# A graph network layer: the last blocks of edges in halves, and the last 512 nodes through a layer with nodes as rows

## The chip, the cores and the metric

One core of one Trainium2 chip. The time is device microseconds of one execution. The profile is of one execution of the kernel before; its lines give microseconds (us) from the first instruction. Engines: PE (matmul; PEld its weight loads), DVE (vector), ACT (scalar), POOL (here: issues the gathers), SP (issues the other transfers). L229 is line 229 of the kernel before.

## What is computed

8192 nodes of 256 features, 131072 edges with 64 features, sorted by their target. All in 32-bit floats.

```python
ea  = edge_attr @ w_e + b_e                       # 131072 x 256
msg = relu(x[src] + ea)
agg = segment_sum(msg, dst, 8192)
h_local = bn1(relu((x + agg) @ w1 + b1) @ w2 + b2 + x)
h_attn  = bn2(attention in groups of 32 nodes, 4 heads, of x @ in_w.T + in_b, then out_w, out_b, + x)
out = h_local + h_attn
out = out + relu(out @ m_w1 + m_b1) @ m_w2 + m_b2
result = layernorm(x + bn3(out))                  # over the 256 features
```

The three `bn` are a scale and a shift per feature (s1, s2, s3; cA and c3 gather the shifts).

## The kernel before

**Edges.** The edges go in 128 blocks of 1024, a block in 4 groups (h) of two tiles (j) of 128 edges. Per block:
- `gather(b)` (L157, POOL): 8 indirect DMAs fetch the source rows, 128 each, into `xs` (four buffers).
- `load_edges` (L173, SP) and `edge_transpose` (L190, DVE): edge features to `eaT`.
- `edge_products(b)` (L208, PE): 8 matmuls to `pe`, two PSUM pairs of banks (2 groups each, `bank2`, two buffers in all, which the attention scores at L474 use too).
- `edge_messages(b)`: DVE adds `pe` and `xs` (L229, one add for each half of a block, 128x1024), ACT takes the relu (L233). The add frees the PSUM pair and the gather buffer.
- `edge_hot(b)` (L241, DVE): one-hot tiles `oh` of the targets within a group.
- `edge_sums` (L250, PE): 8 matmuls with 32 columns each sum the messages by target to `pw`; ACT copies to `ws` (L263), DVE makes `oh2` (L267).
- `edge_place` (L278, PE; L287, DVE): two matmuls place the sums in a window of nodes and add them to `xT`, the transposed x of the 512 nodes concerned.

**Nodes.** 16 chunks of 512 nodes. `attention_front` and `attention_back` (L432 to L527) don't need the edges. `dense` does: once the last block that reaches a chunk is placed, it runs `w1` (ACT relu, L553), `w2` (DVE, hA, L556), `m_w1` (ACT relu, L562), `m_w2` (DVE, zT, L574), all with features as rows, transposes zT back (L583, PE), adds x (L589), takes mean and variance (L591, L592), the root (L595, ACT) and writes y (L601, L606). The last two chunks are run in parts: 256, 256, then four of 128 nodes.

**Order.** PE's order is fixed when the program is built. Up to block 104 (`TAIL`) it follows a simple loop, with node work in between. From there a small planner runs on estimated times: `came[b]` is when a block's gathers should have come, `added` when its messages should be there, and at each step it takes placing, sums, products or messages if their estimated time has come, or else a step of node work (`work.step`). DVE's and ACT's order is chosen by the build's scheduler, which keeps `edge_messages` behind the instructions in `newest` (so far the latest `ws` and the latest `xT`), by `tc.issue_after`. Each engine executes its own order strictly, and waits where an operand isn't there.

**General path.** If the targets don't fit the windows, a register (`width`) sends every engine into a second path (from L853), a loop over all edges and one over all nodes. With these inputs it is jumped over, at the end.

Of the kernel before, what the change touches and what calls it, by code (L numbers as in the profile page):

```python
# [9 lines left out]
FP = mybir.dt.float32  # L10
# [8 lines left out]
P = 128  # L19
# [5 lines left out]
NH = 4  # L25
# [14 lines left out]
ND = 2  # L40
NV = 26
TAIL = 104
AGG_ROWS = N + 2 * P
TE = 8
RS = 1.0 / (1.0 + 1e-5) ** 0.5
LN_EPS = 1e-5
REST = -1.0
# [25 lines left out]
def gnn_kernel(ctx: ExitStack, tc: tile.TileContext, x, src, dst, edge_attr, w, out):  # L73
# [60 lines left out]
    s12 = const.tile([P, KC], FP, name="s12")  # L134
    cA = const.tile([P, KC], FP, name="cA")
    c3 = const.tile([P, KC], FP, name="c3")

    fast = ExitStack()
    epool = fast.enter_context(tc.tile_pool(name="edge", bufs=1))
# [50 lines left out]
        nc.vector.transpose(eaT, ea[:, QR:].rearrange("p (g d) -> p g d", d=ED)[:, :, :QR])  # L190


    pe_of, msg_of, oh_of, newest = {}, {}, {}, {}

    def edge_products(b, pairs=range(0, NH, 2)):

# [19 lines left out]
        if b + 2 < NB:  # L216
            load_edges(b + 2)

    def edge_messages(b):

        xs = xs_of.pop(b)
        msg = msg_of[b] = epool.tile([P, NH, TJ, C], FP, name="msg", tag="msg", bufs=3)
        n = 2 if b < NB - 1 else 1
        for h in range(0, NH, 2):
            pe = pe_of.pop((b, h))
            for u in range(0, 2, n):
                hs = slice(h + u, h + u + n)
                for js in [slice(0, TJ)] if n == 2 or h + u < NH - 1 else [slice(j, j + 1) for j in range(TJ)]:
                    nc.vector.tensor_add(  # L229
                        msg[:, hs, js].rearrange("p u i c -> p i u c"), pe[:, js, u : u + n, :],  # L230
                        xs[:, hs, js].rearrange("p u i c -> p i u c"),
                    )
                    nc.scalar.activation(msg[:, hs, js], msg[:, hs, js], AF.Relu)  # L233
        between()
# [13 lines left out]
    def group_sums(pw, i, b, turns):  # L248
        for h, j in turns:
# [2 lines left out]
                start=(j == 0), stop=(j == TJ - 1), skip_group_check=True,  # L252
            )

    def edge_sums(blocks):

        n = len(blocks)
        pw = pps.tile([P, 2, C], FP, name="pw", tag="pw", bufs=1)
        for i, b in enumerate(blocks):
            turns = [(h, j) for j in range(TJ) for h in range(NH)]  # L260
            group_sums(pw, i, b, sorted(turns) if b == NB - 1 else turns)
# [271 lines left out]
    def dense(n0, st, pool, bank, a=0, z=CH, own=("h1", "m1", "zT", "y", "")):  # L533
# [16 lines left out]

        h1 = pool.tile([P, KC, w], FP, name="h1", tag=own[0])
        for o in range(KC):
            nc.scalar.activation(h1[:, o, :], layer(w1, KC, o, tT), AF.Relu, bias=v_("b1", o))  # L553
            yield 1.7 * part
        for o in range(KC):
            nc.vector.scalar_tensor_tensor(  # L556
                hA[:, o, :], layer(w2, KC, o, h1), s1[:, o : o + 1], hA[:, o, :], op0=ALU.mult, op1=ALU.add
            )
            yield 1.7 * part
        m1 = pool.tile([P, 2 * KC, w], FP, name="m1", tag=own[1])  # L560
        for o in range(2 * KC):
            nc.scalar.activation(m1[:, o, :], layer(mw1, KC, o, hA), AF.Relu, bias=v_("m_b1", o))  # L562
            yield 1.7 * part
        zT = pool.tile([P, KC, w], FP, name="zT", tag=own[2])
        for o in range(KC):
# [5 lines left out]
        st6 = pool.tile([P, TN, 6], FP, name="st", tag="st" + own[4])  # L571
        mv = pool.tile([P, TN, 2], FP, name="mv", tag="mv" + own[4])
        for o in range(KC):
            nc.vector.scalar_tensor_tensor(  # L574
                zT[:, o, :], layer(mw2, 2 * KC, o, m1), s3[:, o : o + 1], zT[:, o, :], op0=ALU.mult, op1=ALU.add
            )
            yield 3.4 * part
        for t2 in range(0, nt, 2):
            n2 = min(2, nt - t2)
# [29 lines left out]
        yield 0.0  # L609


# [31 lines left out]
    class Work:  # L643
# [5 lines left out]
        def __init__(self, n):  # L649
            self.streams = [[] for _ in range(n)]  # L650
            self.rest, self.turn, self.owed = [0] * n, 0, 0.0
            self.at, self.placed_at = [0.0] * n, 0.0

        def add(self, stream, ready, gen):
            self.streams[stream].append((ready, gen))
# [25 lines left out]

        def step(self, t, until):

            n = len(self.streams)
            for i in [k % n for k in range(self.turn, self.turn + n)]:
                while self.streams[i] and self.streams[i][0][0]() and t >= self.at[i]:
                    d = next(self.streams[i][0][1], None)
                    if d is None:
                        self.streams[i].pop(0)
                        self.at[i] = max(self.at[i], self.placed_at)  # L690
                    elif d == REST:
                        self.at[i] = t + 6.0
                    elif d > 0:
                        t += d
                        self.at[i], self.turn = t + 0.5, (i + 1) % n
# [14 lines left out]
    with tc.manual_schedule(engines={PE}):  # L710
# [9 lines left out]
        for c in range(NCH):  # L720
            st, before, same = chunk[c], chunk[c - 1], chunk[c - 4]
            front = attention_front(c * CH, st, npool, bank)
            if c < 2:
                next(front)
            work.add(
                FRONT,
                lambda c=c, b=before, s=same: (c < 1 or b.get("scores"))
                and (c < 4 or s.get("dense")),
                front,
            )  # L730
            work.add(BACK, lambda s=st: s.get("front"), attention_back(st, npool, bank, bank2))
            if c < NCH - 2:
                work.add(DENSE, summed(c), dense(c * CH, st, npool, bank))
        for i, c, a, z in (
            (DENSE2, NCH - 2, 0, CH // 2), (DENSE, NCH - 2, CH // 2, CH), (DENSE2, NCH - 1, 0, P),
            (DENSE, NCH - 1, P, 2 * P), (DENSE2, NCH - 1, 2 * P, 3 * P), (DENSE, NCH - 1, 3 * P, CH),
        ):
            d = dense(c * CH, chunk[c], npool, bank, a, z, *([OTHER] if i == DENSE2 else []))
# [10 lines left out]
        while b < TAIL:  # L749
# [5 lines left out]
            for i in blocks:  # L755
                if i + 2 < NB:
                    gather(i + 2)
                if 4 <= i < 8:
                    wt, name = ((w1, "w1"), (w2, "w2"), (mw1, "m_w1"), (mw2, "m_w2"))[i - 4]
                    nc.sync.dma_start(wt, w[name].rearrange("(k p) m -> p k m", p=P))  # L760

            if b:
                edge_products(b)
                edge_messages(b)
                next_edges(b + 2)
# [23 lines left out]
            b += 2  # L789

        came = [7.9 + 10.035 * (i + 1) for i in range(NB)]
        t, p, m, s, l = came[b - 2] + 20, b, b, b - 2, b - 2
        added = dict((i, came[i] + 2.0) for i in range(b))
        summed_at, bank_free = {}, t
        work.at = [t] * len(work.streams)
        while l < NB:

            times = [1e9] * 4
            if l < s:
                times[0] = summed_at[l] + 1.5  # L800
            elif s < m:
                times[1] = max(added[s] + 1.2, bank_free)
                if s == NB - 1:
                    times[1] = max(came[s] + 2.2, bank_free)
            if p < NB - 1 and m == p:
                times[2] = added[p - 1]
            if m < p:
                times[3] = came[m]
            if t >= times[0]:
                edge_place(*sums)  # L810
                placed = l
                t += 0.75
                bank_free = work.placed_at = t + 0.7
                l += 1
                if l == NB - 1:
                    edge_products(l, [2])
                    edge_hot(l)
                    t += 1.0
                    p += 1
            elif t >= times[1]:  # L820
                sums = edge_sums([s])
                t += 1.2
                summed_at[s] = t
                s += 1
                if s == NB - 1:
                    edge_products(s, [0])
                    t += 1.0
            elif t >= times[2]:
                if p + 2 < NB:
                    gather(p + 2)  # L830
                edge_products(p)
                next_edges(p + 2)
                edge_hot(p)
                t += 2.1
                p += 1
            elif t >= times[3]:

                with ExitStack() as behind:
                    for i in newest.values():
                        behind.enter_context(tc.issue_after(i))  # L840
                    edge_messages(m)
                added[m] = max(t, came[m], added[m - 1] + 0.5) + 2.0
                m += 1
            elif l == s - 1 == NB - 1:
                t = times[0]
            else:
                t = work.step(t, min(times))
        work.finish()
# [124 lines left out]
```

## Time and profile before

| | us |
|---|---|
| median of three runs (1314.24 to 1318.11) | 1315.99 |
| the profiled execution | 1315.85 |
| its span, first to last instruction | 1314.1 |
| busy: PE, DVE, ACT, POOL | 1198.9, 803.9, 592.0, 975.3 |
| mean granted clock of PE | 0.964 |

A group's line gives the mean of one instruction: message add 1214 ns (128x1024), relu 1054, 512-column matmul 595 (they overlap; one of a run of 32-bit matmuls takes two such records, 0.86 us), y add 686 (128x512), statistics 411, aggregate 170. A line of the timeline gives start, length, engine, line, operation and, in brackets, the idle time before and what ended it. A line of waits gives total, number and longest.

### The profile page before, as it was taken

What the parts mean: (1) busy time and instruction counts of PE and PEld (TensorE: products, weight loads), DVE (VectorE), ACT (ScalarE), POOL (GpSimd) and SP (SyncE); (2) the same over time, 40 slices, a digit from 0 to 9 for tenths busy, and PEclk for the clock granted to TensorE, in tenths of its full rate; (3) what the DMA queues carried; (4) which work ended last, traced back from release to release, by engine and by line L of the source; (5) the groups of instructions that cost most, each with busy time, mean ns of one, the idle gap of its engine ahead of it and who ended that gap; (6) DMA issues with size and microseconds to landing.
All of it is one profiled execution on the core that took longest, in us unless ns stands there. A gap on an engine that the chain in (4) does not pass through costs nothing.

```text
span 1314.1 us, 21073 instructions
## 1 busy us (share of the span) xinstructions
PE 1198.9 (91%) x7683; PEld 722.8 (55%) x7683; DVE 803.9 (61%) x1634; ACT 592.0 (45%) x850; POOL 975.3 (74%) x1032
## 2 busy tenths in 40 slices
PE   5987989999999989898997999889898999989986
PEld 3554646556565555555564555545555555555665
DVE  6567665757566565745746574565647558475663
ACT  2524444454545264443544444354454445453443
POOL 7777777777777777777777777777777777777772
PEclk8989999999999989898999999989899999999998
DMA  9999976677666666665767566576566567665741
GB/s 230 280 328 275 280 216 166 175 188 192 169 182 158 171 181 159 188 163 152 195 163 185 153 185 169 154 186 169 169 170 191 149 168 194 162 168 154 193 135 48
DMA packets 148922, 240.35 MB, mean 183 GB/s; under 512 B 27950, under 2 KB 112204, under 8 KB 148044
## 3 DMA queue, kind: packets, MB, share of 16 engines
q0 software_dynamic: 49152, 134.28, 38.6%
q1 hardware_dynamic: 98572, 104.65, 29.4%
q8 instruction: 62, 1.02, 0.3%
q14 instruction: 48, 0.39, 0.1%
q10 hardware_dynamic: 1088, 0.00, 0.0%
HBM read 222.06 MB, written 16.78 MB: 182 GB/s over the span
## 4 chain that ended last, share of the span: by engine, by line
POOL 34%; PE 31%; issue 16%; DMA 9%; DVE 8%; ACT 2%; SPq 0%; DVEq 0%; POOLq 0%; ACTq 0%
POOL xs L157 34%; PE at L546 8%; DMA xs<-xb,srci 6%; PE pe L208 6%; PE at L443 3%; PE pw L250 3%; PE pe L203 2%; PE at L524 2%; DVE msg L229 2%; PE l L278 1%; DVE bd L504 1%; PE at L512 1%; PE at L457 1%; DMA xb<-xp 1%; DVE eaT L190 1%
## 5 line engine op out<-in xcount | busy, mean ns | idle before, releaser
L157 POOL DMA_INDIRECT xs<-xb,srci x864 | 819.1, 948 | 263.2 <-issue 247.7
L233 ACT ACTIVATE msg<-msg 128x1024 f32<-128x1024 f32 (+1 forms) x259 | 270.0, 1046 | 401.4 <-DVE msg L229 397.4
L229 DVE TENSOR_TENSOR msg<-pe,xs 128x1024 f32<-128x1024 f32 (+1 forms) x259 | 306.6, 1207 | 196.5 <-PE pe L208 91.2
L208 PE MATMUL pe<-we,eaT 64*128 64x256 f32 x2048 | 270.3, 401 | 13.5 <-ACT pr L484 9.8
L208 PEld LDWEIGHTS pe<-we,eaT 64*128 64x128 f32 x2048 | 195.4, 194 | 117.9 <-issue 62.8
L157 POOL DMA_INDIRECT xs<-in_x_dram,srci x144 | 138.8, 964 | 43.9 <-issue 40.8
L250 PE MATMUL pw<-msg,oh 128*32 128x256 f32 x2048 | 129.8, 385 | 1.2 <-ACT msg L233 0.8
L546 PE MATMUL at<-hA,mw 128*128 128x512 f32 (+2 forms) x320 | 125.8, 520 | 4.5 <-DVE hA L556 4.3
L443 PE MATMUL at<-xT,inT 128*128 128x512 f32 x256 | 121.8, 602 | 3.2 <-ACT xT L433 3.2
L546 PE MATMUL at<-m,mw 128*128 128x512 f32 (+2 forms) x320 | 119.4, 517 | 0.0
L190 DVE STREAM_TRANSPOSE eaT<-ea 128x512 f32<-128x512 f32 x128 | 90.0, 703 | 22.0 <-PE pe L208 18.6
L250 PEld LDWEIGHTS pw<-msg,oh 128*32 128x32 f32 x2048 | 59.9, 110 | 63.6 <-issue 22.8
L278 PEld LDWEIGHTS l<-oh,ws 128*128 128x128 f32 x512 | 73.7, 195 | 27.3 <-issue 21.4
L278 PE MATMUL l<-oh,ws 128*128 128x160 f32 (+4 forms) x512 | 85.9, 308 | 1.8 <-ACT ws L263 1.7
L546 PEld LDWEIGHTS at<-hA,mw 128*128 128x128 f32 x320 | 55.1, 192 | 53.4 <-issue 41.2
L546 PEld LDWEIGHTS at<-m,mw 128*128 128x128 f32 x320 | 55.7, 192 | 48.0 <-issue 44.8
L443 PEld LDWEIGHTS at<-xT,inT 128*128 128x128 f32 x256 | 46.9, 191 | 57.4 <-issue 47.6
L446 ACT ACTIVATE qk<-at,vec 128x512 f32<-128x512 f32 x64 | 43.8, 685 | 73.7 <-PE at L443 73.6
L546 PE MATMUL at<-xT,w 128*128 128x512 f32 (+2 forms) x160 | 66.3, 551 | 8.8 <-DVE xT L287 8.8
L562 ACT ACTIVATE m<-at,vec 128x512 f32<-128x512 f32 (+2 forms) x80 | 47.9, 599 | 58.5 <-PE at L546 58.0
L546 PE MATMUL at<-h,w 128*128 128x512 f32 (+2 forms) x160 | 65.3, 532 | 9.4 <-ACT oT L519 7.0
L241 DVE TENSOR_TENSOR oh<-iota_n,rel 128x128 f32<-128x128 f32 x256 | 57.6, 279 | 18.2 <-PE pw L250 14.8
(111 smaller groups left out, 1200.7 us busy)
## 6 DMA issues: line engine op xcount, KB each, us to landing
ea<-in_edge_attr_dram SPq DMA_DIRECT2D x512, 128.0 KB
xs<-xb,srci POOLq DMA_INDIRECT x864
xn<-in_x_dram SPq DMA_DIRECT2D x16, 512.0 KB
out_dram<-y SPq DMA_DIRECT2D x14, 512.0 KB
xp<-in_x_dram SPq DMA_DIRECT2D x10, 512.0 KB
xb<-xp SPq DMA_DIRECT2D x10, 512.0 KB
xp<-in_x_dram SPq DMA_DIRECT2D x3, 1024.0 KB
xb<-xp SPq DMA_DIRECT2D x3, 1024.0 KB
```

Source lines behind the costliest of these rows:

```text
L157: nc.gpsimd.indirect_dma_start(out=xs[:, h, j, :], out_offset=None, in_=x if b < NX else xb[:, :], in_offset=bass.IndirectOffsetOnAxis(ap= ...
L190: nc.vector.transpose(eaT, ea[:, QR:].rearrange("p (g d) -> p g d", d=ED)[:, :, :QR])
L208: nc.tensor.matmul(pe[:, i, u, :], eaT[rows, h + u], we[rows, :], start=(b >= NX), stop=True, skip_group_check=True)
L229: nc.vector.tensor_add(msg[:, hs, js].rearrange("p u i c -> p i u c"), pe[:, js, u : u + n, :], xs[:, hs, js].rearrange("p u i c -> p i u c"),
L233: nc.scalar.activation(msg[:, hs, js], msg[:, hs, js], AF.Relu)
L241: nc.vector.tensor_tensor(oh[:, ts], iota_n[:, None, :WN].to_broadcast([P, TB // 2, WN]), rel[:, b, ts, None].to_broadcast([P, TB // 2, WN ...
L250: nc.tensor.matmul(pw[h * WN : (h + 1) * WN, i, :], oh_of[b][:, h * TJ + j, :], msg_of[b][:, h, j, :], start=(j == 0), stop=(j == TJ - 1), ...
L278: nc.tensor.matmul(l2[:, k, at : at + wn], ws[:, i, k * P : (k + 1) * P], oh2[:, i, :wn], start=(i == 0 and k == 0), stop=(i == last), ski ...
L443: nc.tensor.matmul(ps, inT[:, k, o * P : (o + 1) * P], xT[:, k, :], start=(k == 0), stop=(k == KC - 1))
L446: nc.scalar.activation(qk[:, o, :], ps, AF.Identity, bias=v_("in_b", o))
L546: nc.tensor.matmul(ps, wt[:, k, o * P : (o + 1) * P], act[:, k, :], start=(k == 0), stop=(k == nk - 1))
L562: nc.scalar.activation(m1[:, o, :], layer(mw1, KC, o, hA), AF.Relu, bias=v_("m_b1", o))
```

## The change

From block 104 on the planner goes by halves of a block: products, messages and sums of two groups at a time, each with its own due time, messages tried ahead of products. `newest` also holds the latest relu and the latest dense step on DVE. Node work is held to a share of 0.42 of the time between blocks 115 and 124. The last part of chunk 14 is two parts of 128 nodes. The last chunk goes through `dense_rows`: up to the third layer as before, then the fourth layer has the activations as stationary operand, so that nodes are rows; x and the bn3 scale enter by matmuls with `ident` and a diagonal into the same PSUM tile, and statistics and output read PSUM. For that `m_w2` is scaled by s3 once, at block 12 (with c3 as a row), and `dense` adds instead of scaling. In the general path the loop over edges takes one tile a turn. SP's last transfers stand in another order: the output of the first 128 nodes of chunk 14's second half is issued ahead of the last block's last edge load.

```diff
-TE = 8
+SHARE = 0.42
+TE = 1
-    def edge_messages(b):
+    def edge_messages(b, pairs=range(0, NH, 2)):
 ...
-        for h in range(0, NH, 2):
+        for h in pairs:
             pe = pe_of.pop((b, h))
 ...
+    def some_sums(b, groups):
+        if b not in pw_of:
+            pw_of[b] = pps.tile([P, 2, C], FP, name="pw", tag="pw", bufs=1)
+        group_sums(pw_of[b], 0, b, [(h, j) for h in groups for j in range(TJ)])
 ...
     (dense)
-            nc.scalar.activation(h1[:, o, :], layer(w1, KC, o, tT), AF.Relu, bias=v_("b1", o))
+            newest["relu"] = nc.scalar.activation(h1[:, o, :], layer(w1, KC, o, tT), AF.Relu, bias=v_("b1", o)).ins
 ...
-            nc.vector.scalar_tensor_tensor(
-                zT[:, o, :], layer(mw2, 2 * KC, o, m1), s3[:, o : o + 1], zT[:, o, :], op0=ALU.mult, op1=ALU.add
-            )
+            newest["dense"] = nc.vector.tensor_add(zT[:, o, :], layer(mw2, 2 * KC, o, m1), zT[:, o, :]).ins
 ...
+    def dense_rows(n0, st, pool, bank, a, own=("h1", "m1", "zT", "y", ""), ahead=False):
 ...
+        nc.vector.tensor_add(y, st["xn"][:, a // P, :], c3row)
+        def sum_of_x():
+            ps = bank()[:, :C]
+            nc.tensor.matmul(ps, ident, y, start=True, stop=False, skip_group_check=True)
+            return ps
 ...
+        for k in range(KC):
+            nc.tensor.matmul(
+                out_ps[:, k * P : (k + 1) * P], hA[:, k, :], diag[:, k, :], start=False, stop=False,
+                skip_group_check=True,
+            )
+        for k in range(2 * KC):
+            nc.tensor.matmul(
+                out_ps, m1[:, k, :], mw2[:, k, :], start=False, stop=(k == 2 * KC - 1), skip_group_check=True
+            )
+        nc.vector.bn_stats(st6, out_ps)
+        nc.vector.bn_aggr(mv, st6)
+        nc.scalar.activation(rstd, mv[:, 1:2], AF.Sqrt, bias=eps_t)
+        nc.vector.reciprocal(rstd, rstd)
+        nc.vector.tensor_scalar(y, out_ps, mv[:, 0:1], rstd, ALU.subtract, ALU.mult)
+        nc.sync.dma_start(out[ds(n0 + a, P), :], y)
 ...
     (Work.step)
+            if self.paced_from <= t < self.paced_to:
+                self.credit += SHARE * (t - max(self.seen, self.paced_from))
+                self.seen = t
+                if self.credit < -0.02:
+                    return min(until, t - self.credit / SHARE)
 ...
     (the parts of the last chunks)
-            (DENSE2, NCH - 2, 0, CH // 2), (DENSE, NCH - 2, CH // 2, CH), (DENSE2, NCH - 1, 0, P),
+            (DENSE2, NCH - 2, 0, CH // 2), (DENSE, NCH - 2, CH // 2, 3 * P), (DENSE, NCH - 2, 3 * P, CH),
+            (DENSE2, NCH - 1, 0, P),
 ...
     (the planner)
-            if l < s:
-                times[0] = summed_at[l] + 1.5
-            elif s < m:
-                times[1] = max(added[s] + 1.2, bank_free)
+            if l < s[0]:
+                times[0] = summed_at[l] + 0.7
+            elif (s[0], s[1] + (s[0] == NB - 1)) < tuple(m):
+                i, k = s
+                times[1] = max(added[i, k] + 1.2, bank_free)
 ...
-            if p < NB - 1 and m == p:
-                times[2] = added[p - 1]
-            if m < p:
-                times[3] = came[m]
+            if p[0] < NB and (p[0] - 1, p[1]) < tuple(m):
+                times[2] = added[p[0] - 1, p[1]]
+            if tuple(m) < tuple(p):
+                times[3] = came[m[0]] - 2.5 * (1 - m[1])
 ...
             elif t >= times[3]:
                 with ExitStack() as behind:
                     for i in newest.values():
                         behind.enter_context(tc.issue_after(i))
-                    edge_messages(m)
-                added[m] = max(t, came[m], added[m - 1] + 0.5) + 2.0
+                    edge_messages(m[0], (2 * m[1],))
+                added[tuple(m)] = max(t, came[m[0]] - 2.5 * (1 - m[1])) + 1.3
 ...
+            elif t >= times[2]:
+                i, k = p
+                if not k and i + 2 < NB:
+                    gather(i + 2)
+                edge_products(i, (2 * k,))
+                if k:
+                    next_edges(i + 2)
+                else:
+                    edge_hot(i)
+                t += 1.0
```

More of the change, by code (lines that the diff above doesn't have):

```diff
@@ L136, in gnn_kernel @@
     c3 = const.tile([P, KC], FP, name="c3")
+    diag = const.tile([P, KC, P], FP, name="diag")
+    c3row = const.tile([P, C], FP, name="c3row")
     fast = ExitStack()
@@ L253, in group_sums @@
             )
+    def some_sums(b, groups):
+        if b not in pw_of:
+            pw_of[b] = pps.tile([P, 2, C], FP, name="pw", tag="pw", bufs=1)
+        group_sums(pw_of[b], 0, b, [(h, j) for h in groups for j in range(TJ)])
     def edge_sums(blocks):
         n = len(blocks)
[L258 to L261, printed above, removed]
+        pw = pw_of.pop(blocks[0], None)
+        if pw is None:
+            pw = pps.tile([P, 2, C], FP, name="pw", tag="pw", bufs=1)
+            for i, b in enumerate(blocks):
+                group_sums(pw, i, b, [(h, j) for j in range(TJ) for h in range(NH)])
         ws = epool.tile([P, 2, C], FP, name="ws", tag="ws", bufs=2)
@@ L561, in dense @@
         for o in range(2 * KC):
-            nc.scalar.activation(m1[:, o, :], layer(mw1, KC, o, hA), AF.Relu, bias=v_("m_b1", o))
+            newest["relu"] = nc.scalar.activation(m1[:, o, :], layer(mw1, KC, o, hA), AF.Relu, bias=v_("m_b1", o)).ins
             yield 1.7 * part
@@ L733, in gnn_kernel, with banks_of_last @@
                 work.add(DENSE, summed(c), dense(c * CH, st, npool, bank))
+        def banks_of_last():
+            one = bank2()
+            yield one[:, 0]
+            yield bank()
+            yield bank()
+            two = bank2()
+            yield bank()
+            yield two[:, 0]
+            yield two[:, 1]
+            yield one[:, 1]
+            yield bank()
+            yield bank()
+        last_banks = banks_of_last()
         for i, c, a, z in (
-            (DENSE2, NCH - 2, 0, CH // 2), (DENSE, NCH - 2, CH // 2, CH), (DENSE2, NCH - 1, 0, P),
+            (DENSE2, NCH - 2, 0, CH // 2), (DENSE, NCH - 2, CH // 2, 3 * P), (DENSE, NCH - 2, 3 * P, CH),
+            (DENSE2, NCH - 1, 0, P),
             (DENSE, NCH - 1, P, 2 * P), (DENSE2, NCH - 1, 2 * P, 3 * P), (DENSE, NCH - 1, 3 * P, CH),
         ):
-            d = dense(c * CH, chunk[c], npool, bank, a, z, *([OTHER] if i == DENSE2 else []))
+            own = [OTHER] if i == DENSE2 else []
+            if c < NCH - 1:
+                d = dense(c * CH, chunk[c], npool, bank, a, z, *own)
+            elif z < CH:
+                d = dense_rows(c * CH, chunk[c], npool, bank, a, *own)
+            else:
+                d = last_part = dense_rows(c * CH, chunk[c], npool, lambda: next(last_banks), a, ahead=True)
             ready = summed(c, z)
@@ L811, in gnn_kernel @@
                 placed = l
-                t += 0.75
+                t += 0.6
                 bank_free = work.placed_at = t + 0.7
                 l += 1
[L815 to L819, printed above, removed]
-            elif t >= times[1]:
[L821 to L835, printed above, removed]
+            elif t >= times[1]:
+                i, k = s
+                last = range(NH - 1, NH) if i == NB - 1 else range(NH // 2, NH)
+                some_sums(i, last if k else range(last.start))
+                t += 0.14 * TJ * (len(last) if k else last.start)
+                if k:
+                    sums = edge_sums([i])
+                    summed_at[i] = t
+                elif i == NB - 1:
+                    next(last_part)
+                onward(s)
             elif t >= times[3]:
```

86 lines of the change are left out of this document (74 added, 12 removed).

## The prediction

> **What bounds the kernel now.** I read the chain of work that ended last, then POOL's waits.
>
> ```profile
> POOL 34%; PE 31%; issue 16%; DMA 9%; DVE 8%; ACT 2%; SPq 0%; DVEq 0%; POOLq 0%; ACTq 0%
> POOL xs L157 <- issue: 295.8, 963, 2.7
> POOL xs L157 <- DMA xs<-xb,srci: 6.4, 21, 0.3
> ```
>
> POOL issues 1024 gathers, 0.95 us each with 0.30 behind it, and hardly waits for anyone: a block of 8 takes 10.03 us. The kernel is this stream, up to 1290.2 us, and a tail. The change leaves the stream alone. The tail in the timeline:
>
> ```profile
> 1289.26 0.94 POOL L157 DMA_INDIRECT xs<-xb,srci  x1 [0.30 <-issue]
> 1294.62 1.09 PE L250 MATMUL pw<-msg,oh 128*32 128x256 f32 x16
> 1297.01 0.33 DVE L287 TENSOR_TENSOR xT<-l,xT 128x160 f32<-128x160 f32 x1 [2.86 <-PE l L278]
> 1309.12 0.41 DVE L601 TENSOR_SCALAR y<-y,mv,rstd 128x256 f32<-128x256 f32 x1
> ```
>
> Rows land some 2.83 us after their gather starts, the last at 1292.1; y is ready at 1309.5, the span ends at 1314.1. The tail is short only because the message adds have caught up with the gathers by then:
>
> ```profile
> 1148.88 0.95 POOL L157 DMA_INDIRECT xs<-xb,srci  x1 [0.31 <-issue]
> 1161.81 2.34 DVE L229 TENSOR_TENSOR msg<-pe,xs 128x1024 f32<-128x1024 f32 x2
> 1279.25 0.94 POOL L157 DMA_INDIRECT xs<-xb,srci  x1 [0.30 <-issue]
> 1282.08 1.23 DVE L229 TENSOR_TENSOR msg<-pe,xs 128x1024 f32<-128x1024 f32 x1 [1.34 <-DMA xs<-xb,srci]
> ```
>
> Block 113's last rows land at 1151.7 and the second of its two adds starts at 1162.9: a lag of 11.2 us. For block 126 it is 0. What works the lag off is PE, and by the stage table (PE, PEld, DVE, ACT, POOL busy; then clock, DMA share, GB/s) PE has little to spare:
>
> ```profile
> 1050.00:1120.00 70.00, 66.44 (x439) 38.82 (x432) 46.80 (x97) 34.03 (x51) 52.97 (x56) 1.00 0.69 181
> 1120.00:1190.00 70.00, 66.35 (x414) 37.36 (x412) 44.69 (x89) 31.07 (x47) 53.03 (x56) 1.00 0.61 163
> 1190.00:1260.00 70.00, 66.00 (x444) 45.03 (x444) 43.86 (x96) 30.14 (x51) 53.03 (x56) 1.00 0.68 172
> ```
>
> It idles 4 us in 70. Who held it from 1050 to 1290:
>
> ```profile
> PE at L546 <- DVE xT L287: 4.9, 5, 2.7
> PE pe L208 <- DVE msg L229: 2.7, 2, 1.6
> ```
>
> So PE's edge products, which need a PSUM pair that a message add must first empty, waited for an add only twice. That row decides here.
>
> **The orders, written out.** The schedule is fixed when the program is built, so I wrote out both programs from block 104 on: each engine's instructions in its order, each with the mean of its group in the trace, each starting when its engine is free and what it waits for has ended, gathers at the trace's times. For the kernel before this puts all adds within 1 us of the trace and y at 1308.2 (trace: 1309.5). For the changed one:
>
> | PE waits for | before | after |
> |---|---|---|
> | products, for an add | 4 times, 4.0 us | 16 times, 15.4 us |
> | scores, for an add | none | 4 times, 4.5 us |
> | products, for ACT's score copies | 1.8 us | 2.8 us |
> | sums, for relu | 5 times, 3.2 us | 12 times, 5.4 us |
> | layers, for xT | 6.3 us | 2.0 us |
> | all other, to 1285 | 11.1 us | 6.8 us |
> | 1285 to the end | 2.3 us | 8.1 us |
> | sum | 28.7 us | 45.0 us |
>
> One of them by hand. After block 106's sums PE has four 128x512 matmuls of the fourth layer (0.86 each, 3.5), the placing (0.6), then the scores, which take the two PSUM pairs of block 107's products. Each pair is freed by an add, but the adds now carry a wait for the newest "dense" and "relu" instruction, and DVE has them behind zT and xT: zT can start at 3.7 (end of the layer), ends at 4.4 (0.69, the row of y at L589), xT at 4.9 (0.45), the first add at 6.1 (1.21). PE could start the scores at 4.1: 2.0 us idle. Behind zT on DVE stand xT, both adds and the next one-hot tiles; ACT's relus, PE's scores and the products after them wait for those. At the same place before (1077.9) scores follow sums with no wait. Another: with both pairs taken, the products of the next half stand behind an add that DVE has after two y adds (0.69 each), three statistics (0.41) and two or three aggregates (0.17): 4.4 us with the add, 4.1 of them idle PE; the trace has 1.6 there.
>
> Why so often: in halves, PE has 2 products, 2 sums and a placing per block, each tied to a DVE or ACT step of the same half. The order is planned as if adds followed their gathers at once. With a lag of 8 us (trace, block 104), every such pair is a round trip between PE and DVE. The lag then is never worked off: written out, the second adds are 8.1 us late at block 104, 11.8 at 107, 15.0 at 112, 22 to 24 from 113 to 119, 16 at 126. The paced layers between blocks 115 and 124 don't help, since PE waits for adds then, not for layers.
>
> **Part by part**, on the time of PE's last matmul:
> - waits: +16.3 (45.0 less 28.7).
> - last chunk, rows as nodes: per 128 nodes one 256-column matmul for x (0.43) and two by the diagonal (0.44) more, two transposes (0.24) and 0.05 less: 0.6, four times +2.3.
> - more turns between kinds of matmul, 0.03 to 0.09 each (four 0.86 matmuls take 3.53 before another kind, not 3.44), about 3 more a block: +1.5.
> - before, PE runs at half clock from 1283.3 to 1290.1 (below); that cost some 3.4 and is not taken over: -3.4.
> - statistics straight from PSUM: 0.43 and two hops less behind PE's last matmul: -0.5.
> - one tile a turn: the loop isn't run. At the end each engine jumps over it, and the end waits for DVE's jump:
>
> ```profile
> SPq L966 <- DVEq L853: 0.9, 1, 0.9
> ```
>
> DVE's jump over 175 instructions took 3.2 us; ACT's over 114 and SP's over 97 took 0.5. DVE's is now 110: -0.9, bounds -0.9 and 0.
> - at nothing: set-up at block 12 (four transposes, under 2 us of DVE), under the gather stream with four gather buffers of 10 us; tensor_add for zT (0.69 for 0.74); gathers, whose POOL order stays; on SP the output of 128 nodes now ahead of the last edge load, needed 20 us later. Uncovered, each is under 2 us.
>
> The Trainium skill (Runtime: NRT & Kernel Launch, Instruction fetch mechanics) lets a jump stall when its target lies outside the two loaded pages, so by where the pages lie and not by length; then the 0.9 may stay.
>
> Sum: 16.3 + 2.3 + 1.5 - 3.4 - 0.5 - 0.9 = +15.3. On the profiled execution's own 1315.85 (span 1314.1 and 1.75 around it; 0.14 under the median): 1331.2.
>
> **The clock.** PE idled from 1281.3 to 1283.6, and:
>
> ```profile
> 1282.00:1283.00 1.00, 0.00 (x0) 0.00 (x0) 0.92 (x1) 0.00 (x0) 0.69 (x2) 1.00 0.46 131
> 1284.00:1285.00 1.00, 1.00 (x11) 0.50 (x14) 0.83 (x2) 0.40 (x1) 0.75 (x1) 0.50 0.33 78
> ```
>
> 2.3 us of idling brought half clock for 6.8 us, 3.4 us of PE lost. The order written out for after has six waits of 2 us or more (2.0 to 4.1); the one before has four, and the trace shows one fall. I take one fall: +3.4, so 1334.6; bounds none (1331) and three (1341). The Trainium skill (TensorE: Matmul & The Clock Gate, Part 1) asks for a whole idle window of about 3.4 us; this trace fell with 2.3. By that rule at most three of the six waits count, and the time would lie nearer 1331.
>
> **Rivals.**
> - *The lag is worked off as before* (faster). Then the tail counts: sums directly behind the last relu (PE was 1.2 us late at 1294.62), the last part from xT to y by rows in 9.7 us and not 12.2, the jump 0.9: 4.6 us, about 1311. Decides: block 126's second add less than 4 us behind its gather. For it: before does it. Against: the table. 0.09.
> - *Lag and gain cancel*, block 126 about 4 us late: 1316. 0.04.
> - *The gathers stall too*: block b+4 takes b's buffer 28.5 us after b has landed; with the add, a lag over 27 us holds POOL. Written out it peaks at 25.7 (a first add, block 114). Two falls of the clock ahead of it suffice: 1340 to 1347. 0.08.
> - *No gap is long enough to bring half clock*: 1331, as in the sum. It takes 0.25 of the forecast's 0.79.
> - *The jump stays at 3.2 us*: +0.9, inside the range.
>
> **Numbers.** Forecast (lag stays, 1331 to 1341): 0.79, likeliest 1334. Range 1319 to 1344: the low end is the sum with the turns free (1.5), a third of the added waits absent (5.4) and the lag at block 104 some 5 us smaller, as where the clock falls less before it (the clock fell eight times between 600 and 1050). The high end is three falls of the clock and a short stall of the gathers. 0.3% is 4 us, about what a measurement can tell: faster 0.09, same 0.04, slower 0.87.
>
> **What would show it.** Right: the same gather times, second adds 10 us or more late at blocks 107 to 126, far more PE waiting for message adds from 1070 on, PE's last matmul near 1323 to 1328. Wrong: block 126's add right behind its gather, and y before 1306. The jump: SP's wait for DVE gone, 3.7 us and not 4.5 from y to the end.

## The result, and the profile after

The changed kernel takes 1353.06 us (1350.94 to 1354.85), the kernel before 1316.01 us: a ratio of 1.028, interval [1.0259, 1.0302], 37 us more. Its profiled execution took 1353.51 us with a span of 1351.6. The forecast was 1334 with a range to 1344: the right side, but less than half of the loss.

The chain of work that ended last has changed hands: POOL led it before, PE leads it now.

```profile
PE 38%; POOL 26%; issue 12%; DMA 11%; DVE 8%; ACT 3%; SPq 0%; DVEq 0%; POOLq 0%; ACTq 0%
```

The timeline of its end (start, us, engine, line, what; in brackets the idle time before and what ended it):

```profile
1301.14 0.94 POOL L160 DMA_INDIRECT xs<-xb,srci  x1 [0.30 <-issue]
...
1319.79 2.35 DVE L234 TENSOR_TENSOR msg<-pe,xs 128x1024 f32<-128x1024 f32 x2
...
1337.54 0.33 DVE L299 TENSOR_TENSOR xT<-l,xT 128x160 f32<-128x160 f32 x1 [4.91 <-PE l L290]
...
1347.41 0.54 DVE L684 TENSOR_SCALAR y<-pe,mv,rstd 128x256 f32<-128x256 f32 x1
```

The last gather starts at 1301.1, 11.9 us later than before. Block 126's adds start at 1319.8; its last rows landed at 1294.0 (start of the gather at 1291.16 and 2.83), so the second add, at 1320.9, is 26.9 us late, where before it was not late at all. From the last update of xT (1337.9) to y (1347.9) it is 10.1 us, where before it was 12.2, and from y to the end 3.7, where before it was 4.5.

So the new last layer and the shorter jump do nearly what they were costed at (9.7 and 3.7 us). The loss comes ahead of them, and PE's own account shows of what kind it is. Both windows run from the start of block 104's last gather to the end of PE's last matmul (length, busy PE with its instructions, clock, DMA share, GB/s), first before, then after:

```profile
1058.84:1307.42 248.58, 229.96 (x1554) 0.99 0.59 156
```

```profile
1058.40:1346.16 287.76, 264.03 (x1588) 0.98 0.50 134
```

The stretch is 39.2 us longer. PE is idle for 18.6 us before and 23.7 after, only 5.1 more. The other 34.1 us are busy time, with hardly more instructions. The sums alone, line 250 before and line 255 after, from 1058 on (length, busy PE, busy weight loads, clock, DMA share, GB/s):

```profile
1058.00:1350.00 292.00, 30.86 (x416) 12.00 (x416) 0.98 0.51 134
```

```profile
1058.00:1350.00 292.00, 54.51 (x416) 20.41 (x416) 0.98 0.50 133
```

The same 416 instructions, 23.7 us more. Why, and how the waits come on top, is to be seen at block 107 in the timeline of after:

```profile
1089.69 1.14 PE L211 MATMUL pe<-we,eaT 64*128 64x256 f32 x8 [1.30 <-ACT pr L496]
1090.75 1.06 PE L255 MATMUL pw<-msg,oh 128*32 128x256 f32 x8
1091.75 3.70 PE L558 MATMUL at<-m,mw 128*128 128x512 f32 x8
1095.38 1.06 PE L255 MATMUL pw<-msg,oh 128*32 128x256 f32 x8
1096.37 1.13 PE L211 MATMUL pe<-we,eaT 64*128 64x256 f32 x8
...
1102.84 1.19 DVE L234 TENSOR_TENSOR msg<-pe,xs 128x1024 f32<-128x1024 f32 x1
...
1104.09 2.08 PE L211 MATMUL pe<-we,eaT 64*128 64x256 f32 x8 [3.30 <-DVE msg L234]
...
1106.10 1.93 PE L255 MATMUL pw<-msg,oh 128*32 128x256 f32 x8
```

Each half of the sums, 8 instructions, takes 1.06 us. For comparison, a whole block before, and then two other lines of after:

```profile
1276.33 1.07 PE L250 MATMUL pw<-msg,oh 128*32 128x256 f32 x16
```

```profile
1068.67 1.09 PE L255 MATMUL pw<-msg,oh 128*32 128x256 f32 x16
...
1335.30 1.05 PE L255 MATMUL pw<-msg,oh 128*32 128x256 f32 x4
```

A whole block, 16 instructions, takes 1.07. In after, blocks 102 to 104 have their two halves directly behind each other (the line at 1068.67), and both together take 1.09. The last group of block 127 alone, 4 instructions, still takes 1.05. A sum of group h writes the 32 rows of the PSUM tile that belong to h, and these times fit groups that stream side by side, each with its own two tiles behind each other: four groups in the whole, two in a half, one at the end. The time goes by the fullest group, not by the number of tiles, and a half costs as much as the whole when another kind of matmul stands between the two halves. The order within the sums doesn't matter: before, block 127's sums were issued group by group and still took 1.09 (the line at 1294.62 in the prediction).

The second thing to see is the wait. The first half of block 107's products is ready at 1090.8 and its rows landed by then, but the add comes at 1102.84, behind zT, xT and the layer norm of a dense layer on DVE. PE stands for 3.3 us, and then runs at half clock (2.08 and 1.93 us for what takes 1.13 and 1.06).

### The profile page after: what moved, and what is told of

Read it like the earlier page. It is cut to its first block, busy times and chain, and to the rows that moved or that the text cites. A ratio compares the mean times of both kernels' runs of the same rounds, so it can differ in the third digit from the quotient of the medians.

```text
span 1351.6 us, 21137 instructions
## 1 busy us (share of the span) xinstructions
PE 1229.6 (91%) x7719; PEld 732.3 (54%) x7719; DVE 802.0 (59%) x1636; ACT 591.0 (44%) x851; POOL 974.9 (72%) x1032
## 4 chain that ended last, share of the span: by engine, by line
PE 38%; POOL 26%; issue 12%; DMA 11%; DVE 8%; ACT 3%; SPq 0%; DVEq 0%; POOLq 0%; ACTq 0%
POOL xs L160 26%; PE at L558 11%; PE pe L211 7%; DMA xs<-xb,srci 5%; PE pw L255 4%; PE at L455 4%; PE l L290 3%; PE at L536 2%; DVE msg L234 2%; DMA xb<-xp 2%; DMA ea<-in_edge_attr_dram 1%; PE at L469 1%; DMA xs<-in_x_dram,srci 1%; PE at L524 1%; DMA xp<-in_x_dram 1%
## 5 line engine op out<-in xcount | busy, mean ns | idle before, releaser
L234 DVE TENSOR_TENSOR msg<-pe,xs 128x1024 f32<-128x1024 f32 (+1 forms) x259 | 307.2, 1206 | 196.1 <-PE pe L211 86.7
L211 PE MATMUL pe<-we,eaT 64*128 64x256 f32 x2048 | 272.8, 399 | 22.3 <-ACT pr L496 11.7
L211 PEld LDWEIGHTS pe<-we,eaT 64*128 64x128 f32 x2048 | 191.1, 191 | 133.4 <-issue 63.7
L255 PE MATMUL pw<-msg,oh 128*32 128x256 f32 x2048 | 153.2, 384 | 2.8 <-ACT msg L238 2.8
L558 PE MATMUL at<-hA,mw 128*128 128x512 f32 (+2 forms) x272 | 118.3, 558 | 2.5 <-DVE hA L568 2.5
L558 PE MATMUL at<-m,mw 128*128 128x512 f32 (+2 forms) x272 | 111.1, 551 | 0.0
L255 PEld LDWEIGHTS pw<-msg,oh 128*32 128x32 f32 x2048 | 68.2, 110 | 74.0 <-issue 25.4
L558 PEld LDWEIGHTS at<-hA,mw 128*128 128x128 f32 x272 | 47.8, 192 | 51.6 <-issue 42.3
L558 PEld LDWEIGHTS at<-m,mw 128*128 128x128 f32 x272 | 48.6, 192 | 48.1 <-issue 46.0
L558 PE MATMUL at<-h,w 128*128 128x512 f32 (+2 forms) x136 | 60.7, 569 | 8.4 <-ACT oT L531 7.2
L574 ACT ACTIVATE m<-at,vec 128x512 f32<-128x512 f32 (+2 forms) x68 | 43.1, 635 | 54.7 <-PE at L558 54.7
L586 DVE TENSOR_TENSOR zT<-at,zT 128x512 f32<-128x512 f32 (+2 forms) x34 | 21.3, 626 | 75.8 <-PE at L558 75.7
```

Source lines behind the costliest of these rows:

```text
L211: nc.tensor.matmul(pe[:, i, u, :], eaT[rows, h + u], we[rows, :], start=(b >= NX), stop=True, skip_group_check=True)
L234: nc.vector.tensor_add(msg[:, hs, js].rearrange("p u i c -> p i u c"), pe[:, js, u : u + n, :], xs[:, hs, js].rearrange("p u i c -> p i u c"),
L255: nc.tensor.matmul(pw[h * WN : (h + 1) * WN, i, :], oh_of[b][:, h * TJ + j, :], msg_of[b][:, h, j, :], start=(j == 0), stop=(j == TJ - 1), ...
L558: nc.tensor.matmul(ps, wt[:, k, o * P : (o + 1) * P], act[:, k, :], start=(k == 0), stop=(k == nk - 1))
L574: newest["relu"] = nc.scalar.activation(m1[:, o, :], layer(mw1, KC, o, hA), AF.Relu, bias=v_("m_b1", o)).ins
```

## The experiments

Theory A was that matmul work that PE has no room for sets the time; theory B that the waits do, and the longer sums only fill them. All edits are to the changed kernel unless told otherwise, and every comparison is with the kernel before on the same chip (1315 to 1317 us). Runs on chips on which the kernel before itself takes 1962 us and more stand at the end.

**Sums of a block together** (halves of products and adds stay).

```
-                some_sums(i, last if k else range(last.start))
+                if i == NB - 1:
+                    some_sums(i, last if k else range(last.start))
```

> The changed kernel, but both halves of a block's sums are issued together, where the second half stood; products and message adds stay in halves. Theory A (a half of the sums takes the array as long as the whole, 1.06 against 1.07 us, so that the changed order has 23 us more matmul work than PE has room for): busy PE falls by about 22 us, the lag of the adds stays under 30 us, the gathers hardly stall, and the time falls by 10 to 20 us, to 1333 to 1343. Theory B (the waits of the halves set the time, and the longer sums only fill waits that would be there anyway): the waits grow by what the work shrinks, 1348 to 1354.

1340.0 us, ratio 1.0174 [1.0148, 1.0199]: 13 us under the changed kernel, as theory A has it. PE in the same stretch, and its greatest waits:

```profile
1058.40:1332.20 273.80, 242.78 (x1589) 0.98 0.53 142
```

```profile
PE pe L211 <- DVE msg L234: 13.6, 13, 4.1
PE pe L486 <- DVE msg L234: 3.7, 2, 1.9
```

Busy time falls by 21.3 us and idle time rises from 23.7 to 31.0. Of the 23.7 us that the halves of the sums cost in work, the time shows 13: the rest had covered idle time. In the changed kernel the waits of the first of these rows were 8.8 us, 9 times. Both theories hold a part of these 23.7 us, A the larger; 24 us of the loss of 37 are left.

**Sums twice**, the other way round, in the kernel before: each block's sums (102 to 126) are issued twice, the second run starting anew.

```
             turns = [(h, j) for j in range(TJ) for h in range(NH)]
+            if n == 1 and b < NB - 1:
+                group_sums(pw, i, b, turns)
```

> The kernel before, but the sums of each block from 104 to 126 are issued twice (the second run starts the accumulation anew): 1.0 us more matmul work a block, some 23 us in all, in the order of before. Theory A (matmul work that PE has no room for): the lag at block 126 grows from 0 to 10 us or more, 1324 to 1334. Theory B (work falls into waits that are there anyway): the lag is still worked off, 1316 to 1319.

1329.65 us, ratio 1.0113 [1.0096, 1.013]. The sums grew from 30.9 to 51.6 us of PE:

```profile
1058.00:1350.00 292.00, 51.55 (x816) 25.18 (x816) 0.99 0.51 134
```

So 20.7 us of added work became 14.4 us of time, and block 126's second add came 13.9 us late instead of at once. In this order, without any half, nearly the same work costs nearly what the halves of the sums cost in the changed one. The time is the one that theory A gave; the other 6.3 us of the added work fell into time in which PE had been idle.

**No order of the adds behind the layers.** The adds no longer wait in order for the newest relu and dense instruction.

```
-            newest["relu"] = nc.scalar.activation(h1[:, o, :], ...
+            nc.scalar.activation(h1[:, o, :], ...
 (the same at the six other places of newest["relu"] and newest["dense"])
```

> The changed kernel, but the message adds carry no order behind the newest relu and the newest instruction of the dense layers on DVE (they keep that behind the window copy and the update of xT). Theory A: the sums in halves stay, the lag too; 4 to 8 us less, 1345 to 1349. Theory B (adds held behind layers): most of the loss goes, 1325 to 1338.

1345.1 us, ratio 1.0226 [1.0209, 1.0243], 7 to 8 us less than the changed kernel. As theory A expected: while the sums are long, this order is the smaller part.

**Both edits together.**

> The changed kernel with both edits: a block's sums together, and no order of the adds behind the newest relu and dense instruction. If the two parts add up on the 1340 of the run with whole sums alone: 5 to 9 us less, 1331 to 1335; if the order was what is left of the loss: 1316 or less, with block 126's second add right behind its gather; if halves of products and adds are what is left: 1336 to 1341.

1334.0 us, ratio 1.0128 [1.0101, 1.0155]. The two add up: 13 and 6. Block 126's second add is still 21.5 us late, and 18.7 us over the kernel before are left.

**Halves with another written order.** As the last, and the planner's clock for the last blocks starts 17 us behind the gathers of block 102, not 20.

```
-        t, l = came[b - 2] + 20, b - 2
+        t, l = came[b - 2] + 17, b - 2
```

> Halves of products and adds, whole sums, no order behind newest relu and dense instruction, and the planner's clock starts 17 us behind the gathers of block 102, not 20. If the 18 us that this stands above whole blocks come of the written order: it moves by 5 us or more, to 1320 to 1329, and the lag's steps move to other blocks; if halves as such cost it (one more round trip between PE and DVE in each block): 1331 to 1337.

1326.3 us, ratio 1.0086 [1.0065, 1.0107], as expected of the written order. The lag's step at block 107 is gone (from 4.6 to 12.9 us between blocks 106 and 107 there, from 4.2 to 5.9 here); the one at block 113 stays. So some 8 of the 18.7 us hung on where products, layers and adds happened to be written, not on halves. The size is rough: with the clock at 20 one of four executions took 1327.9 us and the others 1333.4 to 1334.8, and by the two ratios it is 5.5 us.

**Whole blocks again**, with all else of the change: the loop over the last blocks is the one of before (products, adds and sums of a whole block, its planned times, no paced stretch).

> The changed kernel with the loop over the last blocks as before (products, adds and sums of a whole block, its planned times, no paced stretch); the new last layer, the smaller parts of the last two chunks, the order behind newest relu and dense, and one tile a turn stay. If the order of adds alone does harm without halves: lag at block 126 some 8 us and 1320 to 1328; if the harm is all in the halves: the lag is worked off and the shorter tail counts, 1309 to 1313.

1329.4 us, ratio 1.0116 [1.0097, 1.0135], just over the upper end of what the order alone was expected to cost, and far from 1309 to 1313. And the same **without the order behind the layers**:

> As the run with whole blocks, and the message adds carry no order behind the newest relu and dense instruction. What is left of the change is the last layer with nodes as rows, the smaller parts of the last two chunks and one tile a turn. If the order of the adds made up the rest of the loss: the lag at block 126 falls from 13.6 to under 6 us and the time to 1311 to 1318, 12 us or more under whole blocks; if smaller parts and the last layer cost it: 1324 to 1329.

1316.0 us, ratio 1.001 [0.9996, 1.0023], block 126's second add 2.1 us late. These two differ only by the order, 13.4 us. What it does is to be seen at block 118, with the order and without it:

```profile
1207.95 2.00 PE L211 MATMUL pe<-we,eaT 64*128 64x256 f32 x16
...
1215.35 0.69 DVE L587 TENSOR_TENSOR zT<-at,zT 128x512 f32<-128x512 f32 x1 [3.37 <-PE at L559]
1215.96 2.35 DVE L234 TENSOR_TENSOR msg<-pe,xs 128x1024 f32<-128x1024 f32 x2
```

```profile
1204.22 2.00 PE L211 MATMUL pe<-we,eaT 64*128 64x256 f32 x16
...
1207.24 1.21 DVE L234 TENSOR_TENSOR msg<-pe,xs 128x1024 f32<-128x1024 f32 x1
...
1211.27 0.69 DVE L587 TENSOR_TENSOR zT<-at,zT 128x512 f32<-128x512 f32 x1 [1.09 <-PE at L559]
```

Without the order the first add starts 1.0 us after the products; with it 6.0 us after, and DVE stands idle for 3.4 of these, waiting for a layer of PE so that it may do zT and then the add. That the planner counted on the layer being done by then is inferred from the order; how far PE was behind its plan wasn't measured.

**Another start of the clock with whole blocks**, in search of a version that beats both.

> As whole blocks without order, and the planner of the last blocks starts its clock 17 us behind the gathers of block 102 and not 20. Another written order of the same work: if the lag is worked off by block 126 (0 to 4 us), the shorter jump counts and it is level with the kernel before or under it: 1309 to 1315; if not, 1316 to 1325.

1315.8 us, ratio 0.9999 [0.9989, 1.0009]. The lag is worked off by block 126 (0.1 us), and still it is level. No version tried here beats the kernel before.

**One tile a turn alone**, in the kernel before (TE = 1).

> The kernel before with one tile a turn in the general path alone (TE = 1), the loop being jumped over. If the jump goes by length: DVE's jump falls from 3.2 us to under 0.5, y to the end from 4.5 to 3.7 us, and 0.9 us less than before (0.07%); if it goes by where the code lies: 3 us again and no difference.

1315.3 us, ratio 0.9996 [0.9984, 1.0008]. The time can't tell 0.07%, the trace can: y to the end is 3.7 us, not 4.5, and SP's wait for DVE behind the jump is short:

```profile
SPq L852 <- DVEq L853: 0.5, 1, 0.5
```

**On the other chips.** Seven of these kernels ran on chips, too, on which the kernel before takes 2020 us (the first four) and 1962 to 1968 us (the others); the edits are those above, and what was expected was written for the 1316 us of the kernel before.

> The changed kernel, but both halves of a block's sums are issued together, where the second half stood; products and message adds stay in halves. Theory A (a half of the sums takes the array as long as the whole, 1.06 against 1.07 us, so that the changed order has 23 us more matmul work than PE has room for): busy PE falls by about 22 us, the lag of the adds stays under 30 us, the gathers no longer stall, and the time falls by 10 to 20 us, to 1333 to 1343. Theory B (the waits of the halves set the time, and the longer sums only fill waits that would be there anyway): the waits grow by what the work shrinks, 1348 to 1354.

2046 us, ratio 1.0138 [1.0063, 1.0213].

> The kernel before, but the sums of each block from 104 to 126 are issued twice (the second run starts the accumulation anew): 1.0 us more matmul work a block, some 23 us in all, in the order of before. Theory A: PE has some 4 us in 70 to spare, the lag at block 126 grows from 0 to 10 us or more, 1324 to 1334. Theory B: the extra work falls into waits, the lag is still worked off, 1316 to 1319.

2053 us, ratio 1.012 [1.0068, 1.0171].

> The changed kernel, but the message adds carry no order behind the newest relu and the newest instruction of the dense layers on DVE (they keep that behind the window copy and the update of xT). Theory A: the sums in halves stay, the lag too; 4 to 8 us less, 1345 to 1349. Theory B: the adds held behind layers were most of the loss; 1325 to 1338.

2037 us, ratio 1.0101 [1.0051, 1.0152].

> The changed kernel with both edits: sums of a block together, and no order of the adds behind the newest relu and dense instruction. Theory A: 5 to 9 us under the run with whole sums alone, 1325 to 1336; what then remains above the kernel before is the waits of halves of products and adds. Theory B: the same as without the order alone, 1325 to 1338. If both parts are all of it: 1316 or less, block 126's second add right behind its gather.

2030 us, ratio 1.0053 [1.0011, 1.0094].

> As the run with whole blocks, and the message adds carry no order behind the newest relu and dense instruction. What is left of the change is the last layer with nodes as rows, the smaller parts of the last two chunks and one tile a turn. If the order of the adds made up the rest of the loss: the lag at block 126 falls from 13.6 to under 6 us and the time to 1311 to 1318, 12 us or more under whole blocks; if smaller parts and the last layer cost it: 1324 to 1329.

1971 us, ratio 1.0015 [0.9975, 1.0056]; twice repeated:

> As the run with whole blocks, and the message adds carry no order behind the newest relu and dense instruction. What is left of the change is the last layer with nodes as rows, the smaller parts of the last two chunks and one tile a turn. If the order of the adds made up the rest of the loss: the lag at block 126 falls from 13.6 to under 6 us and the time to 1311 to 1318, 12 us or more under whole blocks; if smaller parts and the last layer cost it: 1324 to 1329.

1972 us, ratio 1.0028 [0.9997, 1.0059].

> As the run with whole blocks, and the message adds carry no order behind the newest relu and dense instruction. What is left of the change is the last layer with nodes as rows, the smaller parts of the last two chunks and one tile a turn. If the order of the adds made up the rest of the loss: the lag at block 126 falls from 13.6 to under 6 us and the time to 1311 to 1318, 12 us or more under whole blocks; if smaller parts and the last layer cost it: 1324 to 1329.

1971 us, ratio 1.001 [0.9983, 1.0037].

> As whole blocks without order, and the planner of the last blocks starts its clock 17 us behind the gathers of block 102 and not 20. Another written order of the same work: if the lag is worked off by block 126 (0 to 4 us), the shorter tail and jump count and it beats the kernel before: 1309 to 1314; if not, 1315 to 1325.

1967 us, ratio 1.0031 [0.9999, 1.0063].

> The kernel before with one tile a turn in the general path alone (TE = 1), the loop being jumped over. If the jump goes by length: DVE's jump falls from 3.2 us to under 0.5, y to the end from 4.5 to 3.7 us, and 0.9 us less, 1314.4 to 1315.2 where before has 1315.3; if it goes by where the code lies: 3 us again and no difference.

1961 us, ratio 0.9991 [0.9951, 1.0032].

In all of these the adds are 33 us and more behind their gathers all through the last blocks, whatever the kernel, so they say nothing on how a lag comes about, and no reading above rests on them.

## Why the prediction was right or wrong

- *What bounds it, and the side*: right. PE's spare 4 us in 70 decide, the lag of the adds is no longer worked off, and the time goes up. The signs held in kind: second adds 13 to 36 us late from block 107 on, and PE waits 12.5 us for message adds (8.8 for products, 3.7 for scores), where before it waited 2.7. Two signs failed: the gathers didn't keep their times, and PE's last matmul ended at 1346.2, not at 1323 to 1328.
- *The order behind newest relu and dense*: right in mechanism. It costs 13.4 us with whole blocks, 6 with halves and sums together, 7 to 8 in the changed kernel.
- *The sums: the step that failed.* They stood in the sum as waits ("sums, for relu") and, as work, at nothing: written out "with the mean of its group in the trace", half of the instructions had half of the time. They have all of it, 1.06 for 1.07, wherever another kind of matmul stands between the halves: +23.7 us of PE, in a stage of which the prediction itself said that PE has 4 in 70 to spare. It costs 13 us of time (1353 against 1340); with these, the forecast of 1334.6 would have been some 1348. The changed kernel's own planner made the same mistake: it allows 0.56 us for a half of the sums (0.14 for each of four tiles). The Trainium skill (TensorE: Matmul & The Clock Gate, Part 3: Packing small matmuls — row/col tiling) says that matmuls in different 32-wide tiles of the array run side by side, so that a pack takes about as long as one of them. This trace agrees, with 1.07 for four groups and 1.06 for two; the prediction didn't weigh it.
- *Turns between kinds, +1.5*: too small. The products, issued in halves, went from 50.3 to 55.9 us of PE: 8 instructions alone take 1.13, 16 take 2.00. The group's line before and after, from 1058 on:

```profile
L208 PE MATMUL pe<-we,eaT 64*128 64x256 f32 x384 | 50.3, 399 | 4.2 <-DVE msg L229 2.7 <-ACT pr L484 1.5
```

```profile
L211 PE MATMUL pe<-we,eaT 64*128 64x256 f32 x384 | 55.9, 412 | 11.4 <-DVE msg L234 8.8 <-ACT pr L496 2.6
```

- *Waits, +16.3*: PE's idle time grew by 5.1. With the sums together it grew by 12.4 (31.0 less 18.6), so the estimate was fair for the work that it assumed; with more work PE is late itself and waits less. But the order written out had too much idle time from the start: 28.7 us for the kernel before, where the trace has 18.6. The recorded trace of before could have shown this ahead of the result.
- *Last chunk +2.3, and the rest*: 34.1 less 23.7 and 5.6 leaves 4.8 us of busy time for the new layer and the half clock together.
- *Half clock, one fall*: there were two between 1058 and the last layers, 6.8 and 3.4 us long, with 9.3 us of busy PE in them, so an estimated 4.6 us lost, for 3.3 before (6.5 busy) and 3.4 forecast.
- *Statistics from PSUM -0.5, jump -0.9*: nearly right. From PE's last matmul to y it is 2.1 us before and 1.8 after (-0.3), from y to the end -0.9; together 6.7 before and 5.5 after, -1.2 for -1.4. By these terms 39.2 us of the stretch, 0.4 of which is its earlier start, less 1.2, are the 37.5 us of the span.
- *The rival that the gathers stall*: given 0.08, and it came about: the lag reached 36 us, and POOL waited for buffers.

```profile
1186.34 0.94 POOL L160 DMA_INDIRECT xs<-xb,srci  x1 [6.69 <-DVE oh L279]
```

  The buffer's last readers are the adds (DVE's L234 at 1184.88, just ahead of the instruction named). 6.4 us of this wait are beyond the usual 0.30; with 2.9, 2.5 and 0.5 more at blocks 119, 121 and 126, less 0.4 by which the gathers stood earlier, it is the 11.9 us of the last gather. It wasn't the bound: in the end the adds were still 27 us behind the gathers, and PE set the time.
- *The rival that the lag is worked off*: not in this kernel. Where it was worked off with the new last layer (whole blocks, no order), the time was level, not 4.6 us less. From xT to y it took 11.7 us there, not 9.7, since layers of the other parts stand between its steps on PE. From y to the end it was 3.9 us (4.2 with the clock at 17), not 3.7, because SP then waited 0.3 and 0.5 us for another output to land: the jump was short, but only 0.6 and 0.3 of its 0.9 us showed. That rival's time was too good as well.
- *What stays open*: halves of products and adds, without the order and with sums together, still stand 10.5 us over whole blocks (1326.3 against 1315.8, both with the clock at 17). It wasn't taken apart further how much of that is longer products, how much waits. The loss of 37 us is so taken off in steps of 13 (sums), 6 (order behind layers), some 8 (where things are written) and 10.5 (halves of products and adds); the sizes belong to this sequence, for the order behind layers alone cost 6 to 13.4 us depending on the rest.

## What to carry to other kernels

Cutting a step in half halves its time only if the halves fill the engine as the whole did, or follow each other directly: look at which parts of the array the instructions of a group use side by side before charging half of the group's time. An order that keeps work from overtaking can, once the engine runs late, hold back just the work that would catch up. And where an engine has 4 us in 70 to spare, cost the work of a change first and its waits second.

## What the runs showed of the hardware

- Matmuls that use 32 columns each run four side by side, even when issued group after group, and the time goes by the group with the most of them: 8 tiles in four groups 1.07 us, 4 tiles in two groups 1.06, 2 tiles in one group 1.05. In block 127's sums before, the first four instructions start within 0.04 us of each other, the next four 0.24 us after the first; in a half of after it is two and two.
- Half clock without an idle window. Both falls followed stretches of 3.4 us in which PE was busy for about a third (length, busy PE, clock, DMA share, GB/s), then the spell:

```profile
1099.71:1103.12 3.41, 1.07 (x3) 1.00 0.76 196
1103.12:1104.00 0.88, 0.00 (x0) 0.50 1.02 171
...
1185.03:1188.45 3.42, 1.24 (x10) 1.00 0.10 28
1188.45:1191.86 3.41, 3.41 (x18) 0.50 0.40 120
```

  The rule quoted in the prediction from the Trainium skill (TensorE: Matmul & The Clock Gate, Part 1), a whole idle window, would have had neither; here, as before, the trace decides against it. All changes of the clock in after's trace lie on one beat of 3.413 us. Cut into stretches on this beat, the trace has 17 falls, each behind a stretch with PE busy for 4 to 46%; of the stretches at full clock that no fall followed, the first 15 us left out, none was under 44%. In the ten other traces from chips on which the kernel before takes some 1316 us, the falls stand behind stretches with up to 57%, and stretches without a fall begin at 41%. So within these traces it is PE's busy share of the stretch that tells when the clock falls, not idling without a break.
- The jump over the unused path: after the branch DVE is back in 3.2 us over 175 instructions and in 0.6 us over 110; PE's took 3.8 and 3.3 us. The Trainium skill (Runtime: NRT & Kernel Launch, Instruction fetch mechanics) has it go by where the target lies; no run here moved the target without changing the length, so it isn't told apart.
- On two chips every kernel ran half again as long: the mean granted clock was 0.82 to 0.83 in the profiled executions, for 0.964 here, and PE, DVE and ACT stood still together for 10 us and more at a time. In one such stretch (1004.8 to 1014.7 us of the kernel before with sums twice) ACT began its next instruction 9.9 us after its last, with nothing in the trace that it waited for, while POOL's gathers went on, one each 1.25 us. What held them isn't shown.
